# Attention over heads in groups of four tokens instead of eight, tiles taken in pairs

## The chip, the cores and the metric

The kernel runs on one core of a Trainium2 chip. The metric is device time in microseconds (us), the median of several executions; lower is better. Five engines work side by side, each through its own queue in order: TensorE (PE in the profile, with its weight loads as PEld) multiplies matrices into PSUM, VectorE (DVE), ScalarE (ACT) and GpSimd (POOL) do elementwise work, and SyncE (SP) issues the transfers between HBM and SBUF. The kernel lays out PSUM as eight banks of 512 f32 columns on 128 partitions.

## The reference

Four residual layers are applied to `x`, 128 sequences of 64 tokens with 256 features. The one that most of the change touches is the first: attention inside each token, between its 16 heads of 16 features, with one matrix as queries, keys and values.

```python
kx = modulated_linear(x, s, k_aff_w, k_aff_b, k_w, k_b).reshape(B, N, H, D)
scores = jnp.einsum('bnhd,bnjd->bnhj', kx, kx) / math.sqrt(D)
A = jax.nn.softmax(scores, axis=-1)
out = jnp.einsum('bnhj,bnjd->bnhd', A, kx).reshape(B, N, F)
out = modulated_linear(out, s, o_aff_w, o_aff_b, o_w, o_b)
x = x + out
```

The second layer is an adapter with weights of each sequence (256 to 64, relu, 64 to 256). The third normalises `x` in three ways, with gains and offsets looked up by token (a table of 250 rows, two of 5 rows, one of 3), puts the results and three terms of the sequence through a product of 1536 to 256, silu, a product of 256 to 256 and a layer norm. The fourth is a product of rank 30 with factors of each sequence: first 256 to 30, then a shared matrix `V`, 30 to 256.

## The kernel before

Features are split into two halves of 128 (`C`). The 8192 tokens are worked through in 16 blocks of 512 (eight sequences); a block has four tiles of 128 tokens. A prologue computes what depends on the sequences alone, among it the decoder's factors from `W_dec` (L817 to L845).

The order is not written out by hand. Each operation is recorded with a cost, and a planner (`Plan.order`, L122) plays the operations through its costs and tables of ranks (`TURNS`, one number for each operation, one table each for the prologue, the first, second, middle, last but one and last block), gives out buffers as it goes, and emits every engine's instructions in the order so found. On the chip each engine keeps that order and waits where data is late. Attention of one block runs between pieces of the rest of the block before.

One tile's attention is `tile_attention` (L1003). Keys: the tile's 128 tokens times the key weights (L1009), scaled on VectorE into `kxe` (L1017), plus a bias on GpSimd (L1023). `kxe` has 32 columns for each head: the 16 features, a one-hot of the token within its group of eight, and a one. VectorE transposes it in 32x32 squares (L1034) into `kT`; there 32 partitions hold one group row, and 128 columns are eight tokens times 16 heads. `kR` is a copy on ScalarE whose one-hot rows are scaled by 2^60 less 2^60 (L1042), so that scores between different tokens of a group come out hugely negative. `values` (L1052) transposes `kT` on TensorE.

Scores (L1065): 16 products of 128x128, four groups in each of four 32-row parts of the array. Each f32 product becomes two instructions in the profile. They fill `sc`, four PSUM banks of which there is one set. Only 16 of 128 scores in a row belong to the row's own token. VectorE takes row maxima in two halves (L1074), ScalarE doubles them (L1084), TensorE transposes them (L1090), ScalarE and VectorE split them into two bf16 parts (L1097, L1104), and a product with a selector subtracts them inside `sc` (L1115, `shift`). ScalarE takes exponentials (L1129). `result` (L1140) multiplies them by the values in four 32-column parts of the array, into another bank. VectorE transposes that back (L1152) and takes reciprocals of the sums (L1156), GpSimd scales (L1159), TensorE transposes the tile (L1170), and VectorE applies the style (L1175). After four tiles comes the output product (L976).

`rest` (L1310) does the other layers: down (L1324) and up (L1342) of the adapter, transposes of single tiles (L1392), layer norms (`stats`, L461; `rstd`, L466; `offset`, L1370; `normalize`), the per-token gains by one-hot products (L1436, "picks": `gtab` in three bf16 terms on 96 rows, six products of 512 columns a block), the large product (L1463), the small table's product (L1472), the second product (L1508), a last layer norm, transposes (L1534), and the fourth layer's products (L1551, and L1577 in two visits of two 32-row parts). The last block ends in `finish` (L1185). The one-hot table `oh` is made on VectorE from `ids` (L867).

## Time and profile before

| what | time |
|---|---|
| median of 3 runs | 894.84 us (894.71 to 896.06) |
| the profiled execution, first to last instruction | 892.9 us |
| TensorE busy | 828.7 us |
| VectorE busy | 637.5 us |
| GpSimd busy | 609.6 us |
| ScalarE busy | 447.2 us |

The span is of one profiled execution; the runs also hold what lies before its first and after its last instruction. Busy times are unions of the instructions' intervals. A matmul's interval reaches from its start to a modelled end, so that neighbours overlap; the distance between starts tells how long one holds the array. A line in the profile names the kernel's line, the engine and operation, output and inputs, the shapes (for TensorE: rows and columns of the array in use, then the moving operand), the count and times, and, for idle time, who ended it.

### The profile page before, as it was taken

What the parts mean: (1) busy time and instruction counts of PE and PEld (TensorE: products, weight loads), DVE (VectorE), ACT (ScalarE), POOL (GpSimd) and SP (SyncE); (2) the same over time, 40 slices, a digit from 0 to 9 for tenths busy, and PEclk for the clock granted to TensorE, in tenths of its full rate; (3) what the DMA queues carried; (4) which work ended last, traced back from release to release, by engine and by line L of the source; (5) the groups of instructions that cost most, each with busy time, mean ns of one, the idle gap of its engine ahead of it and who ended that gap; (6) DMA issues with size and microseconds to landing.
All of it is one profiled execution on the core that took longest, in us unless ns stands there. A gap on an engine that the chain in (4) does not pass through costs nothing.

```text
span 892.9 us, 23977 instructions
## 1 busy us (share of the span) xinstructions
PE 828.7 (93%) x9752; PEld 533.5 (60%) x9752; DVE 637.5 (71%) x1368; ACT 447.2 (50%) x825; POOL 609.6 (68%) x830
## 2 busy tenths in 40 slices
PE   4769999999999999999999999999999999999886
PEld 3557746566665756666565746666566656565443
DVE  3879857768685868777685858777786858776544
ACT  1454544555464655545555645545555645545241
POOL 5563673949597795959596785959496876946343
PEclk9789999999999999999999999999999999999997
DMA  8768742233424232322434232422334231202000
GB/s 258 208 157 259 243 115 67 73 82 107 117 84 123 68 117 82 99 90 73 117 87 126 81 105 76 116 73 81 108 96 117 84 95 51 83 3 72 1 25 25
DMA packets 62575, 90.24 MB, mean 101 GB/s; under 512 B 6328, under 2 KB 46200, under 8 KB 62464
## 3 DMA queue, kind: packets, MB, share of 16 engines
q1 hardware_dynamic: 57344, 71.92, 28.1%
q0 software_dynamic: 5120, 16.78, 6.1%
q8 instruction: 77, 1.26, 0.6%
q14 instruction: 34, 0.28, 0.1%
HBM read 75.44 MB, written 13.24 MB: 99 GB/s over the span
## 4 chain that ended last, share of the span: by engine, by line
PE 59%; POOL 14%; DVE 12%; ACT 8%; issue 5%; DMA 2%; SPq 0%; DVEq 0%; ACTq 0%; POOLq 0%
PE bank L1463 18%; PE sc L1065 6%; PE bank L1009 5%; PE bank L1140 4%; PE bank L1508 4%; PE bank L976 4%; DVE mt L1074 3%; PE sc L1115 2%; PE bank L1052 2%; PE bank L1436 2%; PE bank L1170 2%; ACT uu L1430 1%; ACT e L1129 1%; ACT uu L1378 1%; PE bank L1427 1%
## 5 line engine op out<-in xcount | busy, mean ns | idle before, releaser
L1129 ACT ACTIVATE e<-sc 128x1024 f32<-128x1024 f32 x128 | 125.7, 1022 | 85.5 <-PE sc L1115 85.5
L1074 DVE TENSOR_REDUCE mt<-sc 128x8 f32<-128x1024 f32 x128 | 152.0, 1205 | 14.9 <-PE sc L1065 14.6
L1159 POOL TENSOR_TENSOR att<-ao,rz 128x256 f32<-128x256 f32 x45 | 28.1, 624 | 75.7 <-DVE rz L1156 67.6
L1445 DVE TENSOR_TENSOR uu<-uu,bank 128x512 f32<-128x512 f32 x96 | 63.6, 678 | 18.0 <-PE bank L1436 17.5
L1009 PE MATMUL bank<-wk,xsT 128*128 128x256 f32 x256 | 69.6, 406 | 1.2 <-POOL xsT L919 1.2
L1463 PE MATMUL bank<-uu,w_s 128*128 128x512 f32 x128 | 66.7, 603 | 1.2 <-DVE uu L1445 1.2
L1463 PE MATMUL bank<-x2T,w_x 128*128 128x512 f32 x128 | 65.3, 608 | 0.0
L1463 PE MATMUL bank<-uu,w_t 128*128 128x512 f32 x128 | 63.3, 604 | 0.6 <-DVE uu L1445 0.3
L976 PE MATMUL bank<-osT,wo 128*128 128x512 f32 x128 | 59.5, 604 | 0.6 <-DVE osT L1175 0.6
L1463 PE MATMUL bank<-uu,w_h 128*128 128x512 f32 x128 | 59.4, 597 | 0.6 <-DVE uu L1445 0.4
L1009 PEld LDWEIGHTS bank<-wk,xsT 128*128 128x128 f32 x256 | 47.9, 198 | 19.2 <-issue 11.1
L1508 PE MATMUL bank<-w,uu 128*128 128x256 f32 x240 | 57.6, 384 | 0.8 <-DVE uu L1481 0.8
L1084 ACT COPY mt<-mt 128x16 f32<-128x16 f32 x64 | 13.1, 204 | 85.5 <-DVE mt L1074 82.0
L463 DVE BATCH_NORM_STATS2 st<-uu 128x6 f32<-128x256 f32 x120 | 48.4, 417 | 10.4 <-ACT uu L1395 7.1
L1023 POOL TENSOR_TENSOR kxe<-kxe,kbr 128x256 f32<-128x256 f32 x64 | 46.9, 733 | 7.8 <-DVE kxe L1017 5.3
L468 POOL TENSOR_SCALAR ry<-mvy 128x4 f32<-128x4 f32 (+1 forms) x18 | 4.2, 234 | 66.4 <-DVE mvy L464 66.3
L950 POOL TENSOR_TENSOR wdn<-gdb,late 128x512 f32<-128x512 f32 x32 | 40.6, 1273 | 11.5 <-PE bank L1324 6.0
L1017 DVE TENSOR_TENSOR kxe<-bank,dmk 128x256 f32<-128x256 f32 x64 | 26.8, 418 | 30.0 <-PE bank L1009 27.7
L1508 PEld LDWEIGHTS bank<-w,uu 128*128 128x128 f32 x240 | 43.1, 190 | 6.9 <-DVE uu L1481 1.0
L934 POOL DMA_INDIRECT pw<-in_pw,idx x39 | 40.1, 1028 | 8.0 <-issue 6.7
L1097 ACT ACTIVATE mX<-bank,early 128x128 bf16<-128x128 f32 x64 | 23.5, 367 | 39.4 <-PE bank L1090 39.4
L964 POOL TENSOR_TENSOR wup<-wup,ubb 128x512 f32<-128x512 f32 x32 | 40.6, 1270 | 3.3 <-DMA ubb<-ugub 1.4
(231 smaller groups left out, 2136.2 us busy)
## 6 DMA issues: line engine op xcount, KB each, us to landing
xT<-in_xT SPq DMA_DIRECT2D x32, 256.0 KB
gdb<-dgdb SPq DMA_DIRECT2D x16, 512.0 KB
ubb<-ugub SPq DMA_DIRECT2D x32, 256.0 KB
wup<-ugub SPq DMA_DIRECT2D x32, 256.0 KB
dmk<-demod_k SPq DMA_DIRECT2D x30, 256.0 KB
out_x<-uu SPq DMA_DIRECT2D x36, 128.0 KB
ud<-uu SPq DMA_DIRECT2D x8, 512.0 KB
uT<-ud SPq DMA_DIRECT2D x16, 256.0 KB
```

What stands on the lines that cost most here:

```text
L463: dve(256, lambda: nc.vector.bn_stats(st.t, x.t), [x], [st])
L950: lambda w=w, dp=dp: nc.gpsimd.tensor_tensor(w(), gdb.t[:, :, 0:64], dp, ALU.mult),
L964: pool(1.25, lambda w=w: nc.gpsimd.tensor_tensor(w(wup), w(wup), w(ubb), ALU.add), [wup, ubb], [wup])
L976: nc.tensor.matmul(ps.t, owT[:, c, bass.ts(oc, 128)], osT.t[:, c, :], start=(c == 0), stop=(c == C - 1))
L1009: nc.tensor.matmul(ps.t[:, :F], xsT.t[:, c, bass.ts(tl, 128)], kwT[:, c, :], start=(c == 0), stop=(c == C - 1))
L1023: lambda: nc.gpsimd.tensor_tensor(kxe.t[:, :, 0:D], kxe.t[:, :, 0:D], heads(kinds["kbr"][0]), ALU.add),
L1065: nc.tensor.matmul(sc.t[:, q, bass.ts(g, 128)], of_g(kT.t)[r, g, :], of_g(kR.t)[r, g, :], start=(g == 0), stop=(g == 3))
L1074: lambda two=two: nc.vector.tensor_reduce(mt.t[:, two, 0:4], sc.t[:, two, :].rearrange("p q (g n) -> p q g n", g=4), AX.X, ALU.max),
L1129: lambda k=k: nc.scalar.activation(es[k].t, sc.t[:, 2 * k : 2 * k + 2, :], AF.Exp, scale=0.25),
L1445: lambda ps=ps, src=src, dst=dst, c=c: nc.vector.tensor_tensor(dst.t[:, c, :], src.t[:, c, :], ps.t, ALU.mult),
L1463: lambda ps=ps, w=w, src=src, fc=fc, c=c, n=n: nc.tensor.matmul(ps.t, w.t[:, c, bass.ts(fc, 128)], src.t[:, c, :], start=(n == 0 and c == ...
L1508: nc.tensor.matmul(ps.t[:, :F], s2.t[:, c, bass.ts(tl, 128)], w2.t[:, c, :], start=(c == 0), stop=(c == C - 1))
```

## The change

Attention works on pairs of tiles (256 tokens) and on groups of four tokens. A product of scores is then 64x64: four 32-row parts and two 64-column parts of the array, eight in all. A pair has 64 of them, and they fill the same four banks as a tile's 16 did. Of 64 scores in a row, 16 belong to the row's own token. The maxima of a pair are laid out for one product with `pm` (two 64-wide identities side by side added) in place of the transpose; `shift` has 32 products of 64 columns, with selectors of 32 rows; `result` has 64 products on two 64-row and four 32-column parts, and it writes into the first two banks of `sc`, which the exponentials have been read from. The keys, their scaling, bias, offset copy, reciprocals, scaling, transposes and style work on a pair at once.

In `rest`, transposes into rows, the table's scaling, the second product's bias and the last layer norm's elementwise work also take two tiles at once. `offset` is one operation on VectorE instead of two on GpSimd. The one-hot tables hold their three bf16 terms in one set of 32 rows, which is repeated on four 32-row parts, so that the two halves of a pick run in two row parts. The last product of the fourth layer runs in four row parts at once, into `sc`, and the output leaves two tiles at a time. Buffers are fewer and larger, the loads of the prologue share one pool of 12 (16 in two pools before), and all the planner's tables are new (left out here).

```diff
-SLOTS_1 = (("att", 2), ("p1", 8))
-SLOTS_2 = (("kT", 2), ("kR", 2), ("v", 1), ("ao", 2), ("tmp", 3), ("pw", 3), ("p2", 8))
-SLOTS_U = 16, 4
...
+PAIRS = NTILE // 2
+QT = 4
+TG = 8
+SLOTS_4 = (("xT", 2), ("xsT", 1), ("osT", 1), ("x1T", 2), ("x2T", 2), ("kT", 1), ("kR", 1), ("ao", 1), ("pw", 2))
+SLOTS_2 = (("v", 2), ("att", 1), ("tmp", 2), ("p2", 12))
+SLOTS_U = 8, 4
+HEIRS_U = ("x2", "x2", "xn", "xn", "h", "h", "x3", "x3")
 HEIRS_V = ("hnT", "xnT", "g", "s2")
-HEIRS_2 = ("pw", "v", "kT", "kR", "pw", "tmp", "ao", "v")
-EARLY_WIDTHS = (B, 8, C, 2, 2, 1, C, C, C, C, 1, 6) + (C,) * 9
+HEIRS_2 = ("x3", "x2", "h", "xn", "x3", "v", "x2", "h", "att", "v", "tmp", "x3")
+EARLY_WIDTHS = (B, QT, C, 2, 2, 1, TERMS, C, C, C, C, 1, 6) + (C,) * 9
 LATE_WIDTHS = (C * 64, F, F, F, F, K3P, C * K3)
 EARLY, LATE = sum(EARLY_WIDTHS), sum(LATE_WIDTHS)
...
+    def by_row(dst, part, x, rows, n, view):
+        ys = terms_of(x, rows, n)
+        dve(
+            n,
+            lambda: nc.vector.tensor_scalar(ys[0].t[:rows, :n], ys[0].t[:rows, :n], termm[:rows, 0:1], None, ALU.mult),
+            [ys[0]],
+            [ys[0]],
...
+            dve(
+                n,
+                lambda t=t, last=last: nc.vector.scalar_tensor_tensor(
+                    view() if last else ys[0].t[:rows, :n],
+                    ys[t].t[:rows, :n],
+                    termm[:rows, t : t + 1],
+                    ys[0].t[:rows, :n],
+                    ALU.mult,
+                    ALU.add,
+                ),
+                [ys[0], ys[t]],
+                [(dst, part)] if last else [ys[0]],
+                pair=True,
+            )
...
         ids = Buf("ids")
-        load(96, 2048, lambda: nc.sync.dma_start(out=ids.t, in_=a["ids"][:, bass.ts(blk, T)]), [], [ids])
+        load(128, 2048, lambda: nc.sync.dma_start(out=ids.t, in_=a["ids"][:, bass.ts(blk, T)]), [], [ids])
         oh = Buf("oh")
-        dve(360, lambda: nc.vector.tensor_scalar(oh.t, ids.t, rowid[:96], None, ALU.is_equal), [ids, early], [oh])
+        dve(360, lambda: nc.vector.tensor_scalar(oh.t, ids.t, rowid, None, ALU.is_equal), [ids, early], [oh])
         dmk = Buf("dmk")
...
+    def pair_attention(b0, pair, xsT, dmk, osT):
+        ps, kxe, kT, kR = Buf("bank"), Buf("kxe"), Buf("kT"), Buf("kR")
...
         def keys():
-            for c in range(C):
-                nc.tensor.matmul(
-                    ps.t[:, :F], xsT.t[:, c, bass.ts(tl, 128)], kwT[:, c, :], start=(c == 0), stop=(c == C - 1)
-                )
...
+            for l, tl in enumerate(tiles):
+                for c in range(C):
+                    nc.tensor.matmul(
+                        ps.t[:, bass.ts(l, F)],
+                        xsT.t[:, c, bass.ts(tl, 128)],
+                        kwT[:, c, :],
+                        start=(c == 0),
+                        stop=(c == C - 1),
+                    )
+        pe(1.74, keys, [xsT, wk, kxed], [ps], [kxe])
...
-        of_g = lambda t: t.rearrange("p (g n) -> p g n", g=4)
-        dve(
-            512,
-            lambda: nc.vector.transpose(kT.t.rearrange("p (g h t) -> p h g t", g=4, t=8), kxe.t),
-            [kxe],
-            [kT],
-        )
-        kR = Buf("kR")
+        cut = lambda t: t.rearrange("p l (g c n) -> p l c g n", g=4, c=2)
+        for l in range(2):
+            dve(
+                512,
+                lambda l=l: nc.vector.transpose(
+                    kT.t[:, l, :].rearrange("p (n h) -> p h n", h=H), kxe.t[:, l, :, :]
+                ),
+                [kxe],
+                [(kT, l)],
+            )
...
-        sc, mt, ps_m, mX, mTb = Buf("sc"), Buf("mt"), Buf("bank"), Buf("mX"), Buf("mTb")
...
+        sc, mr, mt, ps_m, mX, mTb = Buf("sc"), Buf("mr"), Buf("mt"), Buf("bank"), Buf("mX"), Buf("mTb")
         def scores():
-            for g in range(4):
-                for q in range(4):
-                    r = slice(32 * q, 32 * q + D + 8)
-                    nc.tensor.matmul(
-                        sc.t[:, q, bass.ts(g, 128)], of_g(kT.t)[r, g, :], of_g(kR.t)[r, g, :], start=(g == 0), stop=(g == 3)
-                    )
-        pe(1.01, scores, [kT, kR], [sc], [mt], full=0.63, mode=1)
+            for tg in range(TG):
+                for c in range(2):
+                    for q in range(4):
+                        r = slice(32 * q, 32 * q + D + QT)
+                        nc.tensor.matmul(
+                            sc.t[64 * c : 64 * c + 64, q, bass.ts(tg, 64)],
+                            cut(kT.t)[r, tg // 4, c, tg % 4, :],
+                            cut(kR.t)[r, tg // 4, c, tg % 4, :],
+                            start=(tg == 0),
+                            stop=(tg == TG - 1),
+                        )
+        pe(1.05, scores, [kT, kR], [sc], [mr], full=0.6, mode=5)
         for k in range(2):
             two = slice(2 * k, 2 * k + 2)
...
                 lambda two=two: nc.vector.tensor_reduce(
-                    mt.t[:, two, 0:4], sc.t[:, two, :].rearrange("p q (g n) -> p q g n", g=4), AX.X, ALU.max
+                    mr.t[:, two, :], sc.t[:, two, :].rearrange("p q (g n) -> p q g n", g=TG), AX.X, ALU.max
                 ),
...
-            [mt],
-            [mt],
-        )
+                [(mr, k)],
+                more=0.04,
+            )
+        for c in range(2):
+            r = slice(64 * c, 64 * c + 64)
+            act(
+                64,
+                lambda c=c, r=r: nc.scalar.copy(
+                    mt.t[r, :, bass.ts(c, 16)].rearrange("p q (w n) -> p q w n", w=2),
+                    mr.t[r, :, :].unsqueeze(2).to_broadcast([64, 4, 2, TG]),
+                ),
+                [mr],
+                [(mt, c)],
+            )
         pe(
-            0.15,
-            lambda: nc.tensor.transpose(ps_m.t[:, :128], mt.t.rearrange("p q r -> p (q r)"), ident),
+            0.2,
+            lambda: nc.tensor.matmul(
+                ps_m.t[:, :64], mt.t.rearrange("p q r -> p (q r)"), pm, start=True, stop=True
+            ),
             [mt],
             [ps_m],
             [mX, mTb],
         )
...
         def shift():
-            for g in range(4):
+            for tg in range(TG):
                 for q in range(4):
-                    r8 = slice(32 * q, 32 * q + 8)
+                    r = slice(32 * q, 32 * q + 32)
                     nc.tensor.matmul(
-                        sc.t[:, q, bass.ts(g, 128)],
-                        sel[r8, g, :],
-                        mTb.t[r8, :],
+                        sc.t[:, q, bass.ts(tg, 64)],
+                        sel[r, tg, :],
+                        mTb.t[r, :],
                         start=False,
                         stop=True,
                         skip_group_check=True,
                     )
...
-        ps_o, ao, rz, att = Buf("bank"), Buf("ao"), Buf("rz"), Buf("att")
+        ao, rz, att = Buf("ao"), Buf("rz"), Buf("att")
+        placed = lambda: sc.t.rearrange("p c (t l g h) -> p c l g t h", t=QT, l=2, g=4)
...
         def result():
-            for g in range(4):
-                for q in range(4):
-                    nc.tensor.matmul(
-                        ps_o.t[32 * q : 32 * q + 32, bass.ts(g, 128)],
-                        v.t.rearrange("p (g q d) -> p g q d", g=4, q=4)[:, g, q, :],
-                        es[q // 2].t[:, q % 2, bass.ts(g, 128)],
-                        start=True,
-                        stop=True,
-                    )
-        pe(0.92, result, [v, *es], [ps_o], [ao], full=0.92, mode=2)
+            for l in range(2):
+                for g in range(4):
+                    for q in range(4):
+                        for c in range(2):
+                            r = slice(64 * c, 64 * c + 64)
+                            nc.tensor.matmul(
+                                placed()[32 * q : 32 * q + 32, c, l, g, :, :],
+                                vs[l].t[r, :].rearrange("p (g q d) -> p g q d", g=4, q=4)[:, g, q, :],
+                                es[q // 2].t[r, q % 2, bass.ts(4 * l + g, 64)].rearrange("p (t h) -> p t h", t=QT),
+                                start=True,
+                                stop=True,
+                            )
+        pe(1.0, result, [*vs, *es], [sc], [ao], full=0.9, mode=6)
         of_h = lambda t: t.rearrange("p (h n) -> p h n", h=H)
-        dve(
-            512,
-            lambda: nc.vector.transpose(of_h(ao.t), ps_o.t.rearrange("p (g h t) -> p h g t", g=4, t=8)),
-            [ps_o],
-            [ao],
-        )
-        dve(16, lambda: nc.vector.reciprocal(rz.t, of_h(ao.t)[:, :, D + 8]), [ao], [rz], 0.07)
+        for l in range(2):
+            dve(
+                512,
+                lambda l=l: nc.vector.transpose(
+                    of_h(ao.t[:, l, :]),
+                    sc.t[:, 0:2, :].rearrange("p c (t l g h) -> p l h g (c t)", t=QT, l=2, g=4)[:, l],
+                ),
+                [sc],
+                [(ao, l)],
...
         def offset(mv, r, nr):
-            pool(0.24, lambda: nc.gpsimd.tensor_scalar(nr.t, mv.t[:, :, 0], -1.0, None, ALU.mult), [mv], [nr])
-            pool(0.24, lambda: nc.gpsimd.tensor_tensor(nr.t, nr.t, r.t, ALU.mult), [nr, r], [nr])
+            dve(
+                4,
+                lambda: nc.vector.scalar_tensor_tensor(nr.t, mv.t[:, :, 0], -1.0, r.t, ALU.mult, ALU.mult),
+                [mv, r],
+                [nr],
+            )
...
+            def turn(ps=ps, p=p):
+                for l in range(2):
+                    for c in range(C):
+                        nc.tensor.transpose(
+                            ps.t[:, 256 * l + 128 * c : 256 * l + 128 * c + 128],
+                            x2T.t[:, c, bass.ts(2 * p + l, 128)],
+                            ident,
+                        )
+            pe(0.45, turn, [x2T], [ps], [x2[p]])
+            act(512, lambda ps=ps, p=p: nc.scalar.copy(x2[p].t, ps.t), [ps], [x2[p]])
+            for l in range(2):
+                stats(x2[p], lambda p=p, l=l: wide(x2[p])[:, l, :], mv, 2 * p + l)
...
         for j, src, dst in ((1, xnT, gs), (2, xnT, xnT), (0, hnT, hnT)):
+            pss = [Buf("bank") for _ in range(C)]
+            def pick(pss=pss, j=j):
+                for c in range(C):
+                    r = slice(32 * c, 32 * c + 24)
+                    nc.tensor.matmul(pss[c].t, gtab.t[r, bass.ts(j, 128)], oh.t[r, :], start=True, stop=True)
+            pe(0.24, pick, [oh, gtab, src], pss, [dst], full=0.5, mode=1)
             for c in range(C):
-                ps = Buf("bank")
-                pe(
-                    0.27,
-                    lambda ps=ps, j=j, c=c: nc.tensor.matmul(
-                        ps.t, gtab.t[:, j * F + c * 128 : j * F + c * 128 + 128], oh.t, start=True, stop=True
-                    ),
-                    [oh, gtab, (src, c)],
-                    [ps],
-                    [dst],
-                )
...
+            def second(ps=ps, p=p):
+                for l in range(2):
+                    for c in range(C):
+                        nc.tensor.matmul(
+                            ps.t[:, bass.ts(l, F)],
+                            s2.t[:, c, bass.ts(2 * p + l, 128)],
+                            w2.t[:, c, :],
+                            start=(c == 0),
+                            stop=(c == C - 1),
+                        )
+            pe(1.75, second, [s2, w2], [ps], [x3[p]])
+            dve(
+                512,
+                lambda ps=ps, p=p: nc.vector.tensor_tensor(
+                    wide(x3[p]), ps.t.rearrange("p (l f) -> p l f", l=2), both(b2), ALU.add
+                ),
+                [ps],
+                [x3[p]],
+            )
+            for l in range(2):
+                stats(x3[p], lambda p=p, l=l: wide(x3[p])[:, l, :], mvy, 2 * p + l)
...
+        out4 = Buf("sc")
+        def last():
+            for j in range(4):
+                r = slice(32 * j, 32 * j + 32)
+                nc.tensor.matmul(out4.t[:, j, :F], zT.t[r, :], vw[r, :], start=True, stop=True)
+        pe(0.5, last, [zT], [out4], full=0.85, mode=1)
+        for p in range(PAIRS):
+            n = blk * NTILE + 2 * p
+            dve(
+                512,
+                lambda p=p: nc.vector.tensor_tensor(
+                    wide(x3[p]), out4.t[:, 2 * p : 2 * p + 2, :F], wide(x3[p]), ALU.add
+                ),
+                [(out4, p)],
```

## The prediction

> **What bounds the kernel now.** I read the page's totals and slices first, then the stretches, then the order of time on TensorE, then the waits.
>
> ```profile
> PE 828.7 (93%) x9752; PEld 533.5 (60%) x9752; DVE 637.5 (71%) x1368; ACT 447.2 (50%) x825; POOL 609.6 (68%) x830
> PE   4769999999999999999999999999999999999886
> ...
> PEclk9789999999999999999999999999999999999997
> ```
>
> Busy time of each engine in stretches (PE, PEld, DVE, ACT, POOL, then clock, DMA share, GB/s):
>
> ```profile
> 22.00:45.00 23.00, 18.38 (x180) 13.12 (x179) 18.18 (x34) 11.51 (x25) 13.58 (x14) 0.79 0.73 209
> 45.00:67.00 22.00, 14.45 (x192) 11.39 (x191) 16.42 (x29) 11.11 (x25) 13.88 (x15) 0.84 0.61 156
> 67.00:89.00 22.00, 20.59 (x271) 17.72 (x270) 20.95 (x39) 9.47 (x19) 7.57 (x10) 1.00 0.85 257
> 402.00:452.00 50.00, 48.57 (x613) 31.27 (x605) 37.19 (x82) 26.94 (x49) 37.63 (x51) 1.00 0.33 96
> ```
>
> Between about 67 and 860 us TensorE is busy 97 of 100 us at full clock; VectorE and GpSimd stand at 75%. So there TensorE sets the pace, and what counts is how long each burst holds it. A burst's own duration is no measure, as matmuls overlap. I take its slot: its start to the start of the next burst, idle time taken out. TensorE in order of time (start, length, line, shapes, count, [idle before]):
>
> ```profile
> 446.96 1.17 PE L1065 MATMUL sc<-kR,kT 24*128 24x128 f32 x32
> 448.06 1.08 PE L1140 MATMUL bank<-e,p 128*32 128x128 f32 x32
> 449.07 1.15 PE L1324 MATMUL bank<-x1T,wdn 128*64 128x64 f32 x32
> 450.15 0.66 PE L1052 MATMUL bank<-ident,kT 128*128 128x128 f32 x4
> 450.74 1.16 PE L1342 MATMUL bank<-act,wup 64*64 64x64 f32 x64
> 451.83 0.33 PE L1090 MATMUL bank<-ident,mt 128*128 128x128 f32 x1
> 453.00 0.40 PE L1115 MATMUL sc<-mTb,sel 8*128 8x128 bf16 x16 [0.84 <-DVE mTb L1104]
> 453.34 0.44 PE L1170 MATMUL bank<-ident,att 128*128 128x128 f32 x2
> ```
>
> Slots: scores (L1065) 448.06 - 446.96 = 1.10, result (L1140) 1.01, up (L1342) 1.09, shift (L1115) 0.34 us. The same L1115 burst starts one block earlier at 403.34, so a block of four tiles takes 49.66 us. Summed over the twelve blocks of 200 to 800 us, slots per block are: scores 4.40, result 4.06, picks (L1436) 1.63, shift 1.39, last product (L1577) 0.74, transpose of the maxima (L1090) 0.69, all the rest 35.8; idle 1.28. That makes 48.7 + 1.3 = 50.0 for 600/12.
>
> **The change part by part.** The instructions' single starts inside those bursts show how a tiled burst runs. Four matmuls, one per part of the array, start 6.6 ns apart, each with its weight load, and the next four start a round later: 111.5 ns for 128 columns (L1065), 109.5 (L1140), 58.3 for 64 columns (L1342), 56 for 128 bf16 columns (L1115). Around the rounds there is a start-up: 1.10 - 8 x 0.1115 = 0.21 us for scores, 1.01 - 0.876 = 0.13 for result, 1.09 - 16 x 0.0583 = 0.16 for up, 0.34 - 0.225 = 0.12 for shift.
>
> *Scores.* Before, 32 instructions a tile in 8 rounds of 4. After, a pair of tiles has 64 matmuls (128 instructions, two to an f32 matmul) of 64 columns on eight parts: 16 rounds of 8. Eight starts take 8 x 6.6 = 53 ns, just under the 58.3 of the 64-column round, so a round stays 58.3: 0.93 + 0.19 = 1.12 us a pair, 2.24 a block against 4.40: -2.16.
>
> *Result.* Likewise 16 rounds of 8: 0.93 + 0.17 = 1.10 a pair, 2.20 against 4.06: -1.86.
>
> Here a rule speaks against the change. The rows say 17.0 ns for an instruction of 64 columns on four parts (1.09 us / 64). The Trainium skill (TensorEngine Tiling, Instruction Overhead) says that each matmul has about 60 cycles of overhead, so that dividing an already small dimension gains nothing; "TensorE: Matmul & The Clock Gate" (Part 1) gives the floor as about 25 ns from start to start. By it a burst of 128 would take 3.2 us, and scores and result together 12.8 a block instead of 8.46: a loss of 4.3 where I book a gain of 4.0. The trace shows starts 6.6 ns apart, so I go by the rows; no row shows eight parts at work, and the rule stays as a rival.
>
> *Shift.* 32 bf16 matmuls of 64 columns a pair, on four parts: 8 rounds. Nearest row L1115: a round between half of it (29 ns) and all of it (56, if the 128-column weight load sets it). 0.35 to 0.57 a pair; I take 0.36, since the load's own record (93 ns) already overlaps rounds of 56. -0.67 a block, at worst -0.25.
>
> *Maxima.* Two f32 matmuls of 64 columns (two instructions each) for four one-instruction transposes of 128 columns: as many columns in all, so the same slot of 0.17 each, half as often: -0.34.
>
> *Picks.* Three bursts of two row groups for six full products at 0.23 (L1436). One burst is one round of 512 bf16 columns (0.21) plus a start-up of 0.12 to 0.25, and it breaks the run of full-array products: 0.40 x 3 = 1.2 against 1.63: -0.43, from -0.8 to 0.
>
> *Last product.* One visit of four row groups instead of two of two: 2 x 0.213 + 0.13 = 0.56 against 0.74: -0.18. It now writes the score bank.
>
> *Paired keys, transposes, second product:* the same columns, fewer visits; booked at nothing.
>
> Sum: -5.03 for attention and -0.61 for the rest, 5.64 us of a block's 49.66.
>
> *Other engines.* VectorE loses four of eight maxima (1.205 us each: -4.8 a block); pairing turns two operations of 256 columns (0.41 each) into one of 512 (0.68), four times over; it gains three small offset operations (0.17, the row of L464). From 37 it goes to about 31 us a block. Its transposes of the keys write at a new stride, which no row shows: by L1034 0.70 each, and at twice that +2.8 a block, still hidden. ScalarE loses four exponentials of 1.02 and more: 27 to 21. GpSimd loses six offset operations of 0.22 and, where two of 0.73 become one of 1.27 (rows L1023 and L963), some 2: 37 to 34 of the new 44 us, 77%, the nearest to TensorE. None becomes the bound. The moved offset is a new wait: it stands on VectorE between two maxima in the new order and waits for GpSimd's power (1.04 us). If that is late, the second maximum is, and through it the transpose of the maxima on TensorE.
>
> *Waits.* Idle is 1.28 a block, most of it before the shift, here 0.84:
>
> ```profile
> PE sc L1115 <- DVE mTb L1104: 8.4, 10, 0.8
> PE bank L1436 <- DVE mTb L1104: 2.2, 8, 0.3
> ```
>
> In the changed order I set TensorE's work between two attention steps against the chain that must run meanwhile. Scores to maxima: 1.12 + 2.35 (two maxima) + 0.42 + hops 0.5 = 4.4 us against 5.2 and 6.4 us of work. Maxima to shift: 1.17 (451.83 to 453.00) against 3.1 and 1.5. Shift to result: two exponentials and hops, 2.45, against 2.6 and 4.5. Result to the bank's next user, now also the last product: two transposes, 1.6, against 1.76 and 2.2. Nothing is short, but two slacks are under 0.2 us, and the engines are in order. I keep idle at 1.3; bounds 0.5 and 3.3.
>
> *Prologue.* Of the 64 tiles' scores, four start before 67 us, where TensorE idles 23 us and DMA is at 0.6 to 0.8: no gain there. The one-hot tables cost VectorE about 6 us more (masked sums, at 0.7 to 1 us each) and ScalarE 14 copies of 0.40 less; eight tiles' maxima (-9.6 us) cover that. The selector and ids loads grow by 128 and 64 KB at 156 to 257 GB/s, under a microsecond, and hidden behind the weights. The load pool shrinks from 16 slots to 12, so decoder weights come later, while attention of two blocks moves ahead of them. I book nothing, +-8 us.
>
> *Total.* Attention 5.03 x 60/64 x 16 = 75.5; picks and last product 0.61 x 15 = 9.2 (the last block runs on latency). 84.7 off the profiled execution: 892.9 - 84.7 = 808.2. The median shown is 1.9 above the profiled span (894.84 against 892.9): 810.
>
> **The rivals.**
> *Eight parts run as four.* If starts or data paths hold a round of eight to two rounds of four, scores and result take 32 x 58.3 ns + 0.16 = 2.03 a burst, 8.1 a block against 8.46. Left are 0.35 + 1.62: 2.0 x 15 = 30 us; 865. For it: no eight-part row. Against: starts fit into the round.
> *Waits take the gain.* Each microsecond of added idle in a block costs 15 us. One more microsecond gives 825, two 840. For it: pairs are coarser and slacks of 0.2 us. Against: VectorE and ScalarE are relieved by 6 us a block each.
> *The floor decides: slower.* At 25 ns an instruction scores and result lose 4.34, the shift (2 x (0.8 + 0.12) against 1.39) 0.45, and 0.95 of the other gains stands: +3.84 a block, x 15 = +58: 953. It decides from about 19 ns: (8.46 + 1.39 + 0.95) us over 512 + 64 instructions. The up row's 17.0 is not far below that.
> *The whole stays off the path:* the start of the dense stretch is later by what is gained. That needs 85 us more prologue, and nothing in the load list is that long.
>
> **How the numbers follow.** As booked 0.74 (its own range 798 to 822: rounds +0.3 a block, shift and picks +-6 each, prologue +-8); added waits 0.12; eight as four 0.07; floor or another loss 0.07. 798 less 2 to 840 holds the first two cases nearly whole, 0.8 in all. Measurement tells 0.2% (1.8 us) from no change: faster 0.91, same 0.02, slower 0.07.
>
> **What would show it.** Right: blocks of 44 us; scores and result slots of 1.1 us for 128 instructions with rounds of 58 ns; shift 0.36; TensorE still 95% busy from 70 us on; maxima halved on VectorE. Wrong: bursts of 2 us or more, TensorE idle over 2 us a block before the shift or result, a dense stretch that begins after 80 us, or a GpSimd wait ending last.

## The result and the profile after

Beside ten runs of the kernel before on the same chips (896.04 us median), ten of the changed kernel take 906.23 us (900.61 to 913.14): a ratio of 1.0112, 95% interval 1.008 to 1.0144. It is slower by some 10 us where 85 us less were forecast. The profiled execution spans 903.6 us, 10.7 more than before.

The changed kernel's page, its totals and slices, answers to the first fence of the prediction:

```profile
PE 806.2 (89%) x13848; PEld 519.8 (58%) x13848; DVE 571.7 (63%) x1171; ACT 359.5 (40%) x651; POOL 563.3 (62%) x544
...
PE   6678897979999998999999999999999999969795
...
PEclk8868897999999999999999999999999999977887
```

TensorE is busy for only 22 us less, with 13848 matmuls in place of 9752. VectorE and ScalarE are relieved as expected (66 and 88 us), and none of it reaches the end. Its stretches (PE, PEld, DVE, ACT, POOL, then clock, DMA share, GB/s):

```profile
45.00:67.00 22.00, 15.38 (x331) 11.90 (x330) 21.21 (x29) 6.21 (x12) 16.25 (x14) 0.66 0.52 130
67.00:89.00 22.00, 17.87 (x425) 12.40 (x424) 14.17 (x28) 6.95 (x14) 15.97 (x17) 0.89 0.51 158
89.00:111.00 22.00, 19.43 (x351) 14.89 (x351) 18.57 (x28) 7.57 (x16) 6.71 (x7) 0.78 0.44 126
402.00:452.00 50.00, 47.81 (x866) 30.76 (x866) 31.81 (x68) 22.83 (x42) 35.74 (x34) 1.00 0.37 97
```

TensorE is not yet dense from 67 to 111 us, and its granted clock there is 0.78 to 0.89 where it was 1.00. In the steady stretch VectorE stands at 32 us of 50 and ScalarE at 23, as booked. TensorE in order of time, one block of the changed kernel (start, length, line, shapes, count, [idle before]):

```profile
423.18 1.59 PE L1099 MATMUL sc<-kR,kT 20*64 20x64 f32 x128
...
428.29 1.16 PE L1401 MATMUL bank<-act,wup 64*64 64x64 f32 x64
...
432.62 0.41 PE L1161 MATMUL sc<-mTb,sel 32*128 32x64 bf16 x32 [0.28 <-DVE mTb L1150]
...
437.36 0.67 PE L1191 MATMUL sc<-e,p 64*32 64x64 f32 x42
438.45 0.31 PE L1191 MATMUL sc<-e,p 64*32 64x64 f32 x5 [0.41 <-issue]
439.16 0.32 PE L1191 MATMUL sc<-e,p 64*32 64x64 f32 x6 [0.40 <-issue]
439.89 0.33 PE L1191 MATMUL sc<-e,p 64*32 64x64 f32 x5 [0.41 <-issue]
440.63 0.95 PE L1191 MATMUL sc<-e,p 64*32 64x64 f32 x70 [0.40 <-issue]
441.51 1.13 PE L1535 MATMUL bank<-uu,w_t 128*128 128x512 f32 x2
```

The scores (L1099) hold TensorE for 424.70 - 423.18 = 1.52 us a pair. This result burst (L1191) was booked at 1.10 and takes 441.51 - 437.36 = 4.15, with four gaps for which the profile names no releaser ("issue"); each is 0.4 us of idle time, 0.6 us from start to start. Its other burst of the block, earlier, has its neighbour 1.41 us later. Over the whole span the waits of TensorE are headed by those gaps, which the kernel before did not have:

```profile
PE sc L1191 <- issue: 21.4, 49, 0.6
PE sc L1161 <- DVE mTb L1150: 8.1, 13, 2.6
```

GpSimd in order of time, beside that burst, has three of the block's four gathers of table rows:

```profile
436.49 1.10 POOL L951 DMA_INDIRECT pw<-in_pw,idx  x1
437.89 0.95 POOL L951 DMA_INDIRECT pw<-in_pw,idx  x1 [0.30 <-issue]
439.15 0.95 POOL L951 DMA_INDIRECT pw<-in_pw,idx  x1 [0.30 <-issue]
```

48 of these 49 gaps fall together with a gather. Of 24 result bursts between 200 and 800 us, the 18 beside a gather (17 of them with gaps) take 3.13 us from start to next start, the other six 1.41.

The same slots, summed over the whole of both profiled executions, show where the forecast went (us; idle time is kept apart):

| TensorE | before | after | change | booked |
|---|---|---|---|---|
| scores | 71.8 | 51.2 | -20.6 | -32.4 |
| result | 66.3 | 61.4 | -4.9 | -27.9 |
| shift | 22.4 | 12.4 | -10.0 | -10.0 |
| maxima | 11.4 | 7.7 | -3.7 | -5.1 |
| picks | 26.7 | 13.7 | -13.1 | -6.4 |
| last product | 12.1 | 10.6 | -1.5 | -2.7 |
| all the rest | 619.4 | 650.1 | +30.7 | 0 |
| idle | 52.8 | 87.2 | +34.4 | 0 |

Booked is the prediction's sum per block times 15. The changes make +11.3; 0.6 less lies ahead of the first matmul and behind the last. The rest grows most in the large product (L1463, L1535; +13.1), the transposes of L1427 and L1499 (+8.1), the conditioning's products (L478, L479; +5.3) and the transposes of the keys (+4.3).

### The profile page after: what moved, and what is told of

Its sections match the earlier page's. It is cut to its first block, busy times and chain, and to the rows that moved or that the text cites. A ratio compares the mean times of both kernels' runs of the same rounds, so it can differ in the third digit from the quotient of the medians.

```text
span 903.6 us, 31226 instructions
## 1 busy us (share of the span) xinstructions
PE 806.2 (89%) x13848; PEld 519.8 (58%) x13848; DVE 571.7 (63%) x1171; ACT 359.5 (40%) x651; POOL 563.3 (62%) x544
## 4 chain that ended last, share of the span: by engine, by line
PE 56%; DVE 15%; POOL 12%; issue 7%; ACT 5%; DMA 3%; SPq 0%; another core or an unknown queue 0%; POOLq 0%; DVEq 0%; ACTq 0%
PE bank L1535 24%; PE sc L1191 6%; PE sc L1099 3%; DVE kT L1066 3%; PE bank L1029 3%; DVE st L464 3%; PE bank L1580 3%; POOL p L1604 2%; PE bank L1499 2%; PE bank L1085 2%; POOL kxe L1051 2%; POOL p L1607 2%; ACT kR L1074 2%; ACT uu L1442 1%; PE bank L1227 1%
## 5 line engine op out<-in xcount | busy, mean ns | idle before, releaser
L1204 DVE STREAM_TRANSPOSE ao<-sc 128x512 f32<-128x512 f32 x64 | 42.4, 695 | 91.6 <-PE sc L1191 91.6
L1517 DVE TENSOR_TENSOR uu<-uu,bank 128x512 f32<-128x512 f32 x96 | 61.4, 678 | 60.3 <-PE bank L1511 59.9
L1112 DVE TENSOR_REDUCE mr<-sc 128x16 f32<-128x1024 f32 x64 | 76.1, 1215 | 25.1 <-PE sc L1099 25.1
L1051 POOL TENSOR_TENSOR kxe<-kxe,kbr 128x512 f32<-128x512 f32 x32 | 42.8, 1336 | 57.6 <-DVE kxe L1040 49.8
L951 POOL DMA_INDIRECT pw<-in_pw,idx x64 | 65.0, 1016 | 15.1 <-issue 12.6
L1175 ACT ACTIVATE e<-sc 128x1024 f32<-128x1024 f32 x64 | 62.1, 1022 | 30.4 <-PE sc L1161 29.2
L1535 PE MATMUL bank<-uu,w_t 128*128 128x512 f32 x128 | 68.7, 646 | 2.3 <-DVE uu L1517 2.3
L1066 DVE STREAM_TRANSPOSE kT<-kxe 128x512 f32<-128x512 f32 x64 | 64.8, 1037 | 9.2 <-POOL kxe L1051 9.2
L1535 PE MATMUL bank<-x2T,w_x 128*128 128x512 f32 x128 | 68.2, 639 | 1.4 <-DVE uu L1517 1.4
L1535 PE MATMUL bank<-uu,w_s 128*128 128x512 f32 x128 | 66.9, 608 | 0.0
L1099 PEld LDWEIGHTS sc<-kR,kT 20*64 20x64 f32 x4096 | 48.4, 135 | 24.5 <-issue 5.8
L1535 PE MATMUL bank<-uu,w_h 128*128 128x512 f32 x128 | 61.4, 602 | 0.8 <-DVE uu L1517 0.8
L1099 PE MATMUL sc<-kR,kT 20*64 20x64 f32 x4096 | 53.3, 238 | 9.9 <-issue 4.7
L1029 PEld LDWEIGHTS bank<-wk,xsT 128*128 128x128 f32 x256 | 51.1, 206 | 11.4 <-POOL xsT L936 1.9
L1074 ACT ACTIVATE kR<-kT,early 128x1024 f32<-128x1024 f32 x32 | 39.7, 1241 | 44.1 <-DVE kT L1066 42.3
L1504 ACT COPY uu<-bank 128x512 f32<-128x512 f32 x64 | 36.9, 587 | 39.5 <-PE bank L1499 38.3
```

Source lines behind the costliest of these rows:

```text
L951: lambda tl=tl, n=n: nc.gpsimd.indirect_dma_start(out=pw[tl // 2].t[:, tl % 2, :], out_offset=None, in_=a["pw"], in_offset=bass.IndirectOf ...
L1029: nc.tensor.matmul(ps.t[:, bass.ts(l, F)], xsT.t[:, c, bass.ts(tl, 128)], kwT[:, c, :], start=(c == 0), stop=(c == C - 1),)
L1051: lambda: nc.gpsimd.tensor_tensor(kxe.t[:, :, :, 0:D], kxe.t[:, :, :, 0:D], heads(kinds["kbr"][0]).unsqueeze(1).to_broadcast([128, 2, H, D ...
L1066: lambda l=l: nc.vector.transpose(kT.t[:, l, :].rearrange("p (n h) -> p h n", h=H), kxe.t[:, l, :, :]),
L1074: lambda: nc.scalar.activation(kR.t, kT.t, AF.Identity, bias=apart[:, 1:2], scale=apart[:, 0:1]),
L1099: nc.tensor.matmul(sc.t[64 * c : 64 * c + 64, q, bass.ts(tg, 64)], cut(kT.t)[r, tg // 4, c, tg % 4, :], cut(kR.t)[r, tg // 4, c, tg % 4, : ...
```

## The experiments

Three questions had to be told apart: what opens the gaps, what holds a burst at 1.4 to 1.5 us without them, and why the dense stretch starts 34 us later. A ratio below is to the kernel before on the same chip; the changed kernel's own is 1.0112. Three chips were used, one for each group of runs, and on them the kernel before took 900.88 us (the first four runs below), 890.22 (gathers apart, quarters, both, picks in turn) and 898.67 (the last three). This will matter.

**Without gathers, in the changed kernel.** Its gathers are left out for all blocks but the first:

```diff
-                lambda tl=tl, n=n: nc.gpsimd.indirect_dma_start(
+                lambda tl=tl, n=n, blk=blk: blk or nc.gpsimd.indirect_dma_start(
```

> The changed kernel with the four indirect gathers of each block issued for block 0 only: the table rows of blocks 1 to 15 are left out, so the stale rows of block 0 are used. Theory 'gathers starve TensorE': in the changed kernel 18 of 24 result bursts (L1191) of 200 to 800 us run beside a gather and take 3.13 us in place of 1.41, which is 18 x 1.72 / 12 = 2.6 us a block. Without gathers the issue gaps of 0.6 us inside L1191 are gone (under 5 of some 50), a result slot takes 1.4 us, and the kernel takes about 866 us (860 to 878). Rival 'the gaps come from something else (instruction fetch, result banks)': the gaps stay, 900 to 906 us.

Measured: 866.25 us, ratio 0.9623 (0.96 to 0.9646). TensorE's waits and a steady result burst of this kernel:

```profile
PE sc L1191 <- issue: 0.9, 2, 0.5
```

```profile
439.71 1.48 PE L1191 MATMUL sc<-e,v 64*32 64x64 f32 x128
441.12 1.12 PE L1535 MATMUL bank<-uu,w_h 128*128 128x512 f32 x2
```

49 gaps become two, the slot is mostly 1.41 to 1.6, and a steady block takes 44.9 us in place of 48.3. In the changed kernel the gaps come with the gathers.

**Without gathers, in the kernel before.** The same edit there.

> The kernel before with the same gathers left out for blocks 1 to 15. Theory 'gathers starve only a stage that lives on its instruction supply': the four-part bursts of before (L1140 and L1065, 2.0 and 2.2 us a pair) show no gaps beside gathers, so within 4 us of the kernel before, 892 to 897 us. Rival 'gathers slow TensorE or the DMA engines in general': as large a gain as in the changed kernel, 30 us or more.

Measured: 889.39 us, ratio 0.9868 (0.9842 to 0.9894): 11.5 us less, between the theory's 4 and the rival's 30. Its 64 gathers are these:

```profile
L934 POOL DMA_INDIRECT pw<-in_pw,idx x39 | 40.1, 1028 | 8.0 <-issue 6.7 <-POOL uu L1403 0.3 <-DMA dmk<-demod_k 0.3
L934 POOL DMA_INDIRECT p<-in_pw,idx x25 | 25.5, 1020 | 5.5 <-issue 4.0 <-PE bank L826 1.0 <-POOL uu L1409 0.2
```

Of the 128 bursts of scores and results in the kernel before only three run beside a gather, all of them ahead of 175 us, and none of the three has a gap. Without gathers the bursts kept their slots (scores 71.8 and 72.1 us in all, result 66.3 and 65.9). So this pair can't tell whether bursts of 32 are spared: they hardly met a gather. Its steady block falls from 49.66 to 49.2. Gathers cost something apart from the gaps, about a quarter of their cost in the changed kernel; where, the trace doesn't settle.

**More of the burst.** Without gathers, the first tile of the pair is computed a second time at the burst's end:

```diff
-            for l in range(2):
+            for l in (0, 1, 0):
```

> As the changed kernel without gathers (blocks 1 to 15), and the first tile of each pair in the result burst computed twice, at the burst's end: 64 more matmuls with their weight loads per burst, the same output. To be read against the changed kernel without gathers. Theory 'supply': past the first some 50 matmuls of a burst each takes 16.7 ns, so +64 x 16.7 = 1.07 us a burst, 32 bursts, +34 us. Rival 'the array sets it, as the forecast had it' (rounds of eight in 58.3 ns): +8 x 58.3 = 0.47 us a burst, +15 us.

Measured: 933.31 us, 67 more than without gathers, beyond either theory. TensorE in order of time, two of its bursts of 192, one smooth and one not:

```profile
451.44 2.11 PE L1191 MATMUL sc<-e,p 64*32 64x64 f32 x192
453.47 0.70 PE L1535 MATMUL bank<-uu,w_t 128*128 128x512 f32 x1
```

```profile
343.06 1.73 PE L1191 MATMUL sc<-e,p 64*32 64x64 f32 x152
346.96 0.90 PE L1191 MATMUL sc<-e,p 64*32 64x64 f32 x40 [2.17 <-issue]
```

The smooth one takes 2.03 us, 0.62 more than 128 matmuls: 9.7 ns for each of the 64 (each with its weight load). That is neither the array's 7.3 nor my 16.7, so this theory had the right kind and the wrong size; it gives 20 of the 67 us. The single starts agree: the first 32 start in four rounds of eight, which take 80, 56, 55 and 76 ns; of each 32 after them most start 11 and 6 ns apart in turn and the others 16 to 17 ns, some of these two at once, 9.6 to 10.4 ns on average. So eight parts of the array can run at 55 ns a round, but no burst keeps that up past its first 32 matmuls. That those 32 are the ones that had been queued, and that the rest wait for the supply of instructions, is the reading that fits; the queue itself is not in the trace. The other burst shows a second thing. In nine of the 15 bursts between 300 and 700 us TensorE stops for 1.8 to 4.6 us from start to start (in eight inside the burst, in one at its end). No gather is near, but in the DMA view from 343 to 348 us the only large transfer is a packet of 16 KB of instructions:

```profile
q8 instruction: 1, 0.02, 1.8%
```

It starts at 344.08, and matmuls go on at 346.96. 192 matmuls and their loads are 384 instructions in 2 us. The Trainium skill (Runtime: NRT & Kernel Launch, Instruction fetch mechanics) says that instructions come in blocks of 16 KiB, 256 instructions, and that the fetch is mostly hidden since they are issued more slowly than they are fetched. Here the smooth burst was issued at 5.3 ns an instruction. That these waits are for the fetch is inferred from the packet's place; the changed kernel, with bursts of 128, has only a few long gaps that look like them (the longest 2.9 us).

**The decoder's weights first.** The forecast's eye was on loads that come late. On SyncE's queue the `W_dec` loads stand behind loads of later blocks, which wait for buffers; the first is issued at 98.7 us.

```diff
+    decoder = [o for o in plan.ops if o["tag"] == "W_dec"]
+    for o in plan.ops:
+        if o["tag"] == "later":
+            o["deps"].add(decoder[-1]["n"])
```

> The changed kernel, where the planner may issue the loads of gdb, wup and ubb of blocks 1 to 15 only after the last load of the decoder's weights (W_dec). Theory 'SP's order makes the start late': the first W_dec load is issued before 80 us (98.7 in the changed kernel), the dense stretch of block 0 (L1535 there) starts at 115 to 130 us in place of 146.8, and the kernel takes 15 to 30 us less, 876 to 891 us. Rival 'the start is late because its own products and copies take longer': the dense stretch starts at 140 us or later, within 6 us of the changed kernel.

Measured: 1063.72 us, ratio 1.1764 (1.1687 to 1.1841). The dense stretch starts at 161.0 us and TensorE idles 185.9 us. The new dependency made the planner order everything anew, in every block, and SyncE, in order, stands longest before a load that waits for a late product and before stores of late results:

```profile
SPq L927 <- PE bank L1642: 222.7, 12, 30.4
SPq L1683 <- DVE p L1674: 136.6, 10, 36.1
```

It tells nothing of the first loads by themselves, but much of the planner. The edits below, but for one, leave its order alone and move finished instructions.

**The gathers put apart.** Every engine keeps its order, but GpSimd issues a block's gathers where TensorE has no long burst:

```diff
+        moved = [o for o in done if o["tag"] == "gather" and o["blk"] == blk]
+        for tag, part in (("att", moved[:2]), ("kb", moved[2:])):
+            at = next((i for i, o in enumerate(done) if o["tag"] == tag and i > at), use + 1)
...
+            done[at + 1 : at + 1] = part
```

> The changed kernel with all its work, every engine's order as it was, but the four gathers of a block (blocks 1 to 15) are issued later on GpSimd: two behind the product by 1/z (L1215) that follows the block's second result burst, two behind the next bias add of the keys (L1051), where TensorE has no burst of more than 32 matmuls. Theory 'a gather beside a burst starves it': under 8 of the 0.6 us gaps in the result bursts are left (49 in the changed kernel), and the time is that of the run without gathers plus the 5 to 10 us that the gathers themselves were worth in the kernel before, 868 to 878 us. Rival 'the gathers cost by their number, wherever they stand' (descriptors, DMA engines): 895 to 906 us.

Measured: 868.97 us, ratio 0.9767 (0.9728 to 0.9807), with all its work done. That is 3.45% or 31 us below the changed kernel's ratio, and 2.3% below the kernel before. The steady block is 44.9 us. TensorE and, after it, GpSimd in order of time:

```profile
434.85 1.68 PE L1196 MATMUL sc<-e,v 64*32 64x64 f32 x128
436.46 1.98 PE L1542 MATMUL bank<-uu,w_h 128*128 128x512 f32 x4
```

```profile
438.45 1.05 POOL L1221 TENSOR_TENSOR p<-ao,rz 128x512 f32<-128x512 f32 x1 [3.91 <-DVE rz L1217]
439.67 1.09 POOL L953 DMA_INDIRECT pw<-in_pw,idx  x1 [0.17 <-issue]
```

The burst is whole, the first gather follows it by 3 us. Two gaps are left in result bursts. The changed kernel itself was not run on this chip, so the 31 us rest on the ratios; the last run below repeats the place on another chip, with the offset moved, and comes to the same ratio (0.9759). The 13 us between this and the kernel without gathers are near the 11.5 that they cost in the kernel before.

**The burst in quarters.** Gathers stay; large products that stood ahead of a result burst are put between its quarters of 32 matmuls:

```diff
+        parts = [dict(o, emit=lambda o=o, k=k: o["emit"](k)) for k in ((0,), (1,), (2,), (3,))]
...
+        done[i : i + 1] = [x for n, y in enumerate(parts) for x in ([y] + between[n : n + 1])]
```

> The changed kernel with all its work and its gathers where they were; the result burst is cut in quarters of 32 matmuls, and up to three large products (L1535) that stood ahead of it on TensorE are put between the quarters (in blocks 3 to 14 one burst of a block is cut in four, the other in 32, 32 and 64). Theory 'a burst lives on the instructions already queued, 32 matmuls of them, and on what is refilled while it runs': a quarter goes at 6.7 to 7 ns a matmul whether a gather runs or not, since the queue fills during the 0.4 us of a large product; four quarters take 0.95 us in place of 1.41, the gaps beside gathers go (2.6 us a block, less what still hits the burst of 64), in all 40 to 50 us, 856 to 868 us. Rival 'a gather blocks TensorE itself, or the memory that it writes': the gaps stay, 900 us or more.

Measured: 927.84 us, ratio 1.0428 (1.0381 to 1.0474). The time missed by 60 us and more; the gaps are gone. TensorE, then GpSimd:

```profile
393.40 0.46 PE L1193 MATMUL sc<-e,p 64*32 64x64 f32 x32 [1.52 <-ACT e L1176]
393.78 1.12 PE L1540 MATMUL bank<-uu,w_t 128*128 128x512 f32 x2
394.84 0.45 PE L1193 MATMUL sc<-e,p 64*32 64x64 f32 x32
```

```profile
392.65 1.10 POOL L952 DMA_INDIRECT pw<-in_pw,idx  x1
394.06 0.95 POOL L952 DMA_INDIRECT pw<-in_pw,idx  x1 [0.30 <-issue]
```

Both quarters run through beside a gather (0.39 and 0.38 us to their neighbours); of this line's waits for "issue", 21.4 us in 49 gaps, 0.8 us in two are left. That this is the quarters' doing is not shown, because on this chip whole bursts hardly met such gaps either (the picks in turn and the last run, below). What speaks against a gather that blocks the array is in the changed kernel's own trace: the burst at 437.36 begins while a gather is running (436.49 to 437.59), and its first 42 matmuls go through without a gap. That a gather holds back the refill of TensorE's instructions fits this; no run shows it. The time went into the edit itself. The first quarter now comes ahead of up to three large products, too early for its exponentials (a wait of 44.0 us in all on ScalarE's `e`), and a quarter takes 0.38 us up to its neighbour, four of them 1.52 where the whole burst took 1.41.

**Both.**

> The gathers put apart and the result burst cut in quarters, together. Theory 'one cause, two cures': the 39 us of the gaps are won once, not twice, and the cut alone adds some 0.35 us for each of 24 to 32 bursts, so 8 to 10 us below the kernel with the gathers put apart, 860 to 868 us. Rival 'two causes': 40 us and more below it, under 835 us.

Measured: 928.61 us, ratio 1.043 (1.0393 to 1.0467). It fell with its base, the quarters. Beside the quarters alone (1.0428), putting the gathers apart is worth nothing. Either the cut had already taken away what they cost by their place, or on this chip they cost little there anyway; the run cannot tell.

**The picks in turn.** Row groups undone; both picks then read rows 0 to 55, so that each adds both tables and the picked factors are others:

```diff
-                    r = slice(32 * c, 32 * c + 24)
+                    r = slice(0, 56)
```

> The changed kernel, but both one-hot picks of a pair (L1511) use rows 0 to 55 in place of 24 rows each in groups of their own: they can no longer run at the same time, and each adds both tables, so the picked factors are others. Theory 'the picks gain by their row groups': a pair takes 0.55 us as before in place of 0.28, 48 pairs, +13 us, 916 to 922 us. Rival 'they gain by smaller weights or fewer waits': within 4 us of the changed kernel.

Measured: 985.21 us, ratio 1.1053 (1.1009 to 1.1097). The picks' own slots rise as expected, 13.7 to 28.3 us; the rest is something else. TensorE, VectorE and GpSimd in order of time:

```profile
433.76 0.69 PE L1134 MATMUL bank<-pm,mt 128*128 128x64 f32 x2 [8.94 <-ACT mt L1125]
```

```profile
421.93 9.27 DVE L1433 SCALAR_TENSOR_TENSOR nrh<-mvh,rh 128x4 f32<-128x4 f32 x1
431.12 1.21 DVE L1112 TENSOR_REDUCE mr<-sc 128x16 f32<-128x1024 f32 x1
```

```profile
421.38 1.25 POOL L980 TENSOR_TENSOR wup<-wup,late 128x512 f32<-128x512 f32 x1
...
429.92 1.25 POOL L981 TENSOR_TENSOR wup<-wup,ubb 128x512 f32<-128x512 f32 x1
431.35 1.08 POOL L951 DMA_INDIRECT pw<-in_pw,idx  x1 [0.17 <-issue]
```

The moved offset, 128x4 elements, takes 9.27 us and ends when GpSimd's unbroken row of products ends; behind it stands the second maximum, behind that the transpose of the maxima, and with it TensorE. The path behind the offset is the one that the prediction named. What holds it is not: the prediction had it wait for GpSimd's power, and here the instruction itself stands for the length of that row. In the changed kernel it did little: that line loses 10 us in 47 instructions, and the longest takes 1.9 us.

**The picks in turn, offset on GpSimd.**

```diff
-                lambda: nc.vector.scalar_tensor_tensor(nr.t, mv.t[:, :, 0], -1.0, r.t, ALU.mult, ALU.mult),
+                lambda: (
+                    nc.gpsimd.tensor_scalar(nr.t, mv.t[:, :, 0], -1.0, None, ALU.mult),
+                    nc.gpsimd.tensor_tensor(nr.t, nr.t, r.t, ALU.mult),
+                ),
```

> The kernel with its picks in turn (985 us; both tables added into each pick), and the small offset -mean/std (L1433, 128x4) computed by two instructions of GpSimd, as in the kernel before, in place of one on VectorE; all orders else unchanged. In the run with the picks in turn this one instruction took up to 10.5 us on VectorE (least 0.13), 91 us in all, and ended when a row of products on GpSimd ended. Theory 'VectorE's small instruction stood behind GpSimd's row': the 9 us waits go, 890 to 922 us. Rival 'the picks themselves cost it, the long instruction is only a symptom': 970 us or more.

Measured: 928.24 us, ratio 1.0343 (1.0318 to 1.0367); seven points of the ratio less, some 63 us. The long waits go (TensorE's 78.4 us before L1134 become 6.7). The gaps of the gathers are back, though, 16.7 us of them for 0.9, on another chip. It was not the place: with the picks in turn, ten of the 32 result bursts stand beside a gather, the eight steady ones with gathers as in this run to within 0.2 us. There such a burst goes through in 1.8 to 1.9 us; here the like take 3.5 to 4.0, and all 18 beside a gather have gaps. Against the changed kernel, 2.3% or 21 us remain, of which the picks' slots are 14.4.

**True costs for the planner**, on the kernel with the gathers put apart; each transpose of the keys is given 0.34 us more as well (left out here):

```diff
-        pe(1.05, scores, [kT, kR], [sc], [mr], full=0.6, mode=5)
+        pe(1.52, scores, [kT, kR], [sc], [mr], full=0.6, mode=5)
...
-        pe(1.0, result, [*vs, *es], [sc], [ao], full=0.9, mode=6)
+        pe(1.41, result, [*vs, *es], [sc], [ao], full=0.9, mode=6)
```

> The kernel with the gathers put apart (869 us), its order planned anew with the costs that the trace shows: scores 1.52 in place of 1.05 us, result 1.41 in place of 1.00, each transpose of the keys 0.34 us more. Theory 'the planner's wrong costs cause the idle time that is left' (68 us in that run, 53 in the kernel before; most of it before 150 and after 750 us): 15 us less idle, 850 to 860 us. Rival 'the order written by hand in the table of turns sets it, and any new order is worse': 875 us or more.

Measured: 1026.61 us, ratio 1.144 (1.1386 to 1.1495). The rival holds: the ranks in the table of turns belong to one set of costs, and with others TensorE idles 170.9 us, 81 of them between 202 and 802 us, where blocks take 37 to 66 us from shift to shift.

**Gathers apart, offset on GpSimd:** the two-line edit shown above on that kernel.

> The kernel with the gathers put apart (869 us), and the small offset (L1433 of the changed kernel) on GpSimd as in the kernel before. There its long runs on VectorE are 8 us in all, at most 1.2 us each, and TensorE waits for none of them by name. Theory 'in the changed kernel the move of the offset costs nothing': 866 to 872 us. Rival 'it delays the chain of the layer norm and with it TensorE': 860 us or less.

Measured: 875.86 us, ratio 0.9759 (0.9738 to 0.9781), against 0.9767 with the offset on VectorE: no difference in the ratio, though the forecast of 866 to 872 us was missed by 4 us, on a chip where the kernel before is slower by 8. In the changed order the moved offset costs nothing that can be seen across the two chips.

This pair also shows what the chip adds. Some 720 us in, the two kernels have a burst of scores with the same gathers around it, begun 1.37 us before it and 0.08 us before it. First with the offset on VectorE (TensorE, then GpSimd), then with it on GpSimd:

```profile
719.66 1.65 PE L1104 MATMUL sc<-kR,kT 20*64 20x64 f32 x128
...
719.58 0.96 POOL L953 DMA_INDIRECT pw<-in_pw,idx  x1 [0.30 <-issue]
```

```profile
726.06 1.05 PE L1104 MATMUL sc<-kR,kT 20*64 20x64 f32 x42
727.53 1.19 PE L1104 MATMUL sc<-kR,kT 20*64 20x64 f32 x86 [0.41 <-issue]
...
725.99 0.95 POOL L953 DMA_INDIRECT pw<-in_pw,idx  x1 [0.30 <-issue]
```

On the first chip the burst goes through, on the second it runs dry after some 40 matmuls. Of 14 bursts of 128 beside a gather in the traces of the first chip none has a gap of 0.6 us (a burst of 64 in the prologue stops once, for 1.8 us); on the second all 20 have gaps, as have 18 of 19 in the changed kernel's trace. A gather beside a burst is thus not enough for the gaps by itself. What else it takes stays open, and so does whether it belongs to the chip: no changed kernel ran on both.

## Why the prediction was wrong

The forecast missed by 95 us (from 84.7 less to 10.7 more, profile to profile). By the table and the runs it divides so, to within some 2 us:

- **"I keep idle at 1.3", and the result at 1.10: 31 us.** This step failed first. I looked for waits between the engines that hand data to each other, and GpSimd's gathers hand nothing to attention. They stood in the profile of before as 64 instructions of 1.0 us, and only three bursts of scores or results there, of 32 matmuls each, met one. After, a result burst beside them costs 1.72 us more. Shown: without gathers the gaps vanish; with the gathers moved, the ratio falls from 1.0112 to 0.9767, and to 0.9759 on a chip where gathers do open gaps. Not shown: the path from a gather to TensorE, and whether shorter bursts would have been spared.
- **"Eight starts take 8 x 6.6 = 53 ns, just under the 58.3 of the 64-column round, so a round stays 58.3": 23 us.** Right for two of a burst's first four rounds (55 ns; the other two took 76 and 80), wrong beyond them, where eight starts take some 78 ns. The 6.6 ns were read within rounds of four, in bursts of 16 to 64 matmuls. The row that was long enough, up (L1342, 64 matmuls on four parts), could not tell: its rounds of 58.3 ns leave 14.6 ns for each, more than the 9.7 measured beyond the first 32. Scores took 1.52 and result 1.41 for the booked 1.12 and 1.10; 11.8 and 11.1 us in all. The rule that I weighed against this, some 25 ns from start to start, was far too slow, but it pointed the right way: to a cost for each instruction, not for its columns.
- **"... booked at nothing": 31 us.** The stages that were to stay as they were hold TensorE longer. In part it is their neighbours: in both kernels a large product takes about 430 ns up to the next start, and mostly 520 to 530 beside a burst of small tiles (ahead of it or behind it). The changed order sets more such bursts among the large products, so that between 200 and 800 us one takes 469 ns on average for 449, 0.6 us a block. In part it may be the clock: 0.66 to 0.89 from 45 to 111 us and 0.73 to 0.77 after 802, where in the kernel before it was 1.00 from 67 to 852. How the 31 us divide was not tried.
- **The prologue, "+-8 us".** The dense stretch starts at 146.8 us, not at 113.2. By slots TensorE did 24.5 us more work ahead of it (scores of 12 tiles, not of 7), and idled 9.0 us more. Most of the late start is thus work done earlier, which the 15 blocks behind it don't have to do (694.7 us of slots for 742.0). Idle time at both ends, up to 202 and after 752 us, is 24 us above before; inside, without the gaps, it is 8 below: 16 us of the miss. Whether the late decoder weights cause the first part stays open, since the run that was to show it reordered everything.
- **What held.** These take some 4 us off the miss. The shift came to the booked value. The picks gained 13.1 us where I gave 6.4, and the run that undoes them gives that back: a pair takes 0.28 us, little above the 0.21 of one round, where I had added a start-up and a break for 0.40. No engine took TensorE's place, and the relief of VectorE and ScalarE had the size forecast. The transposes of the keys at their new stride take 1.04 us for 0.70, half of what I allowed, still hidden.

Of the rivals, "waits take the gain" came nearest, with a wait that it did not name: the gaps and what they stretch cost 2 us a block on average (31 / 15), which by that rival alone gives 840. With the gathers apart a steady block takes 44.9 us; 44.0 was forecast. That this is so near is in part luck: scores and result still take 1.6 us a block more than booked, and idle time of 0.3 to 0.4 where 1.3 was kept and cheaper picks make up for most of it. The ends were not forecast.

## What to carry to other kernels

Here a burst of small matmuls ran at the array's rate at its start alone: 6.7 ns from start to start, and 9.7 beyond the first 32. Before a burst is made longer, price what is beyond its start from a burst that is long enough to show it and short enough in columns. Then ask which engines run beside it, even those that exchange no data with it. And measure an effect and its cure on the same chip: here two cures were tried where the effect itself hardly appeared. Where a planner sets the order, move finished instructions to test a cause: a new dependency or a truer cost gives another schedule, and its time answers another question.

## What the runs showed that was not expected

- About 9.7 ns for a matmul with its weight load after the first 32 of a burst on eight parts; those start 6.7 ns apart within a round of eight.
- Beside indirect gathers on GpSimd (1.0 us each) TensorE's bursts can run dry after some 42 matmuls: gaps of 0.6 us from start to start with five or six matmuls between them. It was seen in the changed kernel's trace and in all such bursts on one of the chips, and hardly on another; the path is not shown.
- Nine of 15 bursts of 384 instructions stop for 1.8 to 4.6 us, with a packet of instructions under way within some 2 us.
- A VectorE instruction of 128x4 elements, usually 0.15 us, took up to 10.5 us beside an unbroken row of GpSimd products. The Trainium skill (SBUF — State Buffer, Who interferes with whom) says that a VectorE instruction with two inputs in SBUF contends with a GpSimd instruction that reads SBUF; that the second is blocked for the whole of the other it says of VectorE's two-port modes. This trace agrees that they contend, and adds that the wait can last for a whole row of GpSimd instructions: eight products in the case shown.
